# Graph products woven into the start of the attention steps, one probe for the threshold, three blocks ahead instead of four

## Chip, cores and metric

The kernel runs on one core of one Trainium2 chip. The metric is the device time of one execution in microseconds (us), as the median of several runs. The engines are called PE (TensorE, with its weight loads as PEld), DVE (VectorE), ACT (ScalarE), POOL (GpSimd) and SP (SyncE, which here issues DMAs).

## The reference

There are 4096 nodes with 256 features, and a dense 0/1 adjacency matrix `adj` of 4096 x 4096 with about 1.5% ones. Two layers follow each other; each adds its result to its input and works on `h = relu(layernorm(x))`.

Layer 0 is graph attention with four heads: per head `e = leaky_relu(src_i + dst_j)`, masked by `adj`, softmax over j, times the projected features, then a layer norm.

Layer 1 is a diffusion in two steps (`STEPS` = 2), over a fixed graph and over an attention that is recomputed in each step:

```python
R = S + eye; R = R / R.sum(-1)              # S is the adjacency
Xf = Xa = X
for n in range(2):
    A = top_p_attention(Xa, W1, W2, W3)     # 4096 x 4096, row-stochastic
    Xf = R @ Xf                             # "hop" n of the graph products
    Xa = A @ Xa
    Z  = Z + Xf @ U1[n].T + Xa @ U2[n].T
return layernorm(X + Z)
```

`top_p_attention` makes queries and keys of 64 dimensions, logits `q @ k.T`, a softmax, and keeps in every row the largest probabilities until they sum to 0.9 (`TOP_P`); the rest is set to zero and the row is normalized again. No sort is needed: for every row the kernel looks for the threshold above which the kept values hold 0.9 of the sum.

## The kernel before

Rows are worked on in `NB` = 32 blocks of 128. The program goes through these stages one after the other:

1. Layer 0's preparation (normalization, projections, the tiles `parts`, six buffers, stored to `uv_d` by DMAs of ACT's queue) and its 16 passes of masked products. The adjacency is loaded, cut to one byte per entry and kept in `adj_d`. The closing of the last pass's rows is held in a list `later` and laid between the first products of the next stage.
2. The two hops `R @ Xf` (from L431). The result of a hop is made transposed, in four passes of 1024 columns, each over 32 row blocks j; one (pass, j) is a **piece** of eight matmuls (L459). `before_products` prepares a piece two pieces ahead (`LOOK` = 2): a load of `at` (SP, one for two pieces), a DVE cast to `ar` (L445), an ACT copy to `hl` (L451, high part) and a POOL subtraction (L452, low part); `ar` and `hl` have three buffers each. `drained` copies a pass's four accumulators out and stores them by DMAs of ACT's queue to `xft_d`; after hop 0 `by_rows` also turns them back to rows in `xf_d`, the source of hop 1. Both hops are done before step 0 begins.
3. For each of the two steps: `projections` (keys and queries of all blocks; per-row tables such as the mean and spread of the logits, the shift `nm` and the first guess `c1` of the threshold), then the first blocks, then 32 blocks in a loop.

What happens to one block b of a step:

- `began` gives it a tile `e` of 128 x 4096 (five buffers); `logits` (PE, L540) and `exponentials` (ACT, L672) fill it in four chunks and leave the sum of each.
- `first_probe` (ACT, L679, four instructions of 128 x 2048): what lies below `c1`.
- `first_step` (POOL, from L703): some sixteen instructions on single columns, powers among them, make the next guess from the sums and the probe.
- `second_probe` (DVE pass over the block, L734, and POOL instructions from L735), in step 0 only: a second guess corrected by a secant.
- `third_probe` (DVE pass, L755): what lies below the last guess `c3`, kept in `big`.
- `candidates` (DVE, L768 to L785): the largest values below the guess, 8 of each segment of `big` (16 segments in step 0, 18 in step 1); the threshold is found among the best 48.
- `masked` (DVE pass, L791): values below the threshold become zero.
- `attend` (PE): for eight groups of four, `turn` transposes (L854) and ACT copies to `eT` (L856), then `gather` multiplies with X (L862). Between the groups stand the logits of the block that is `AHEAD` = 4 blocks ahead, its exponentials (groups 0 and 1) and its first probes (groups `PROBED` = 2, 3, 5, 6).
- `finish` (DVE): the block's contribution to Z; in step 1 also the last norm.

The order on PE, DVE, ACT and POOL is written out by hand (`manual_schedule`): each of these engines executes its instructions in the order of the program. In the loop, `chosen_kept(b)` and `attend(b)` alternate:

```python
second_probe(b+1); candidates(b); first_step(b+2)
third_probe(b+1); finish(b-2); masked(b)        # then attend(b)
```

If a row's threshold stays undecided (`questioned` looks at the end of a step), `repaired` does its block again after the step, with a search.

Of the kernel before, what the change touches and what calls it, by code (L numbers as in the profile page):

```python
# [11 lines left out]
F32 = mybir.dt.float32  # L12
# [25 lines left out]
SEG = (16, 18)  # L38
# [5 lines left out]
AHEAD = 4  # L44

PROBED = (2, 3, 5, 6)
# [4 lines left out]
def gat_then_top_p_diffusion(  # L51
# [67 lines left out]
    X = xp.tile([P, NB, D], F32, name="X")  # L119

# [38 lines left out]
    with tc.tile_pool(name="l0", bufs=1) as l0, tc.tile_pool(name="l0s", bufs=2) as l0s, tc.tile_pool(name="l0o", bufs=1) as l0o:  # L159
# [23 lines left out]
        with tc.tile_pool(name="l0r", bufs=3) as rows, tc.tile_pool(name="l0w", bufs=1) as l0w, \  # L183
# [4 lines left out]
            for k in range(KC):  # L188
                for i in range(2):
                    pr = l0w.tile([P, H, HD], F32, name="pr")  # L190
                    nc.vector.tensor_mul(pr, wx[:, k, :D].rearrange("p (h d) -> p h d", h=H),
                                         a_r[:, None, ts(i, HD)].to_broadcast([P, H, HD]))
                    nc.vector.reduce_sum(wx[:, k, ds(D + i * H, H)], pr, axis=AX.X)
            for g in range(NB // 4):
                nc.sync.dma_start(X[:, ts(g, 4), :], x[ts(g, 4 * P), :].rearrange("(b p) d -> p b d", p=P))
            for g in range(NB // 4):
# [5 lines left out]
                for i in range(4):  # L202
# [6 lines left out]
                    hT = rows.tile([P, KC, P], F32, name="hT")  # L209
# [12 lines left out]
                    parts = rows.tile([P, H, 2, W3 + 1], BF16, name="parts", bufs=6)  # L222
# [208 lines left out]
        with tc.tile_pool(name="rp", bufs=2) as rp, tc.tile_pool(name="psr", bufs=1, space=PSUM) as psr, \  # L431
                tc.tile_pool(name="psrt", bufs=2, space=PSUM) as psrt, tc.manual_schedule(engines=every):
            PASSES = NB // G0

            def before_products(hop, p, j, at, rows_):

                q = j % 2
                if q == 0:
                    at[:] = [rp.tile([P, 2, G0 * P], F8, name="at")]
                    nc.sync.dma_start(at[0], adj_d[p, :, ds(j, 2), :])  # L440
                    if hop > 0:
                        rows_[:] = [rp.tile([P, 2, D], F32, name="src")]
                        nc.sync.dma_start(rows_[0], xf_d[ds(j, 2)].rearrange("b p d -> p b d"))
                ar = rp.tile([P, G0 * P], F32R, name="ar", bufs=3)
                nc.vector.tensor_copy(ar, at[0][:, q, :])  # L445
                if j // G0 == p:
                    own = ar[:, ts(j % G0, P)]
                    nc.vector.tensor_tensor(own, own.bitcast(F32), ident, ALU.add)
                src = rows_[0][:, q, :] if hop > 0 else X[:, j, :]
                hl = rp.tile([P, 2, D], F32R, name="hl", bufs=3)  # L450
                nc.scalar.copy(hl[:, 0, :], src)  # L451
                nc.gpsimd.tensor_tensor(hl[:, 1, :], src, hl[:, 0, :].bitcast(F32), ALU.subtract)  # L452
                return ar, hl

            def graph_products(p, j, acc, ar, hl):
                for s in range(KC):
                    for c in range(2):
                        for t in range(2):
                            nc.tensor.matmul(acc[s][c], hl[:, t, ts(s, P)], ar[:, ts(c, 512)],  # L459
                                             start=(j == 0 and t == 0), stop=(j == NB - 1 and t == 1))  # L460

            def drained(hop, p, acc):

                turns = []
                out_ = [rp.tile([P, KC, 512], F32, name="xft") for c in range(2)]
                for s in range(KC):
                    for c in range(2):
                        (nc.vector.tensor_copy if c else nc.scalar.copy)(out_[c][:, s, :], acc[s][c])
                for c in range(2):
                    b = p * G0 + 4 * c  # L470
                    for s in range(KC):
                        nc.scalar.dma_start(xft_d[hop][ds(b, 4), :, s, :].rearrange("b p i -> p b i"),
                                            out_[c][:, s, :].rearrange("p (b i) -> p b i", b=4))

                def by_rows(c, i0):
                    pt = psrt.tile([P, 4, P], F32, name="tp")
                    for i in range(2):
                        for s in range(KC):
                            nc.tensor.transpose(pt[:, KC * i + s, :], out_[c][:, s, ts(i0 + i, P)], ident)
                    row = rp.tile([P, 2, D], F32, name="row")  # L480
                    for i in range(2):
                        b = p * G0 + 4 * c + i0 + i
                        nc.scalar.activation(row[:, i, :], pt[:, ds(KC * i, KC), :].rearrange("p s d -> p (s d)"), AF.Copy,
                                             scale=rinv[:, b:b + 1])
                    nc.scalar.dma_start(xf_d[ds(p * G0 + 4 * c + i0, 2)].rearrange("b p d -> p b d"), row)
                return [lambda c=c, i=i: by_rows(c, i) for c in range(2) for i in (0, 2)] if hop + 1 < STEPS else []

            for hop in range(STEPS):
                at, rows_, ready, turned = [], [], {}, []
                order = [(p, j) for p in range(PASSES) for j in range(NB)]  # L490
                for n in range(len(order) + LOOK):
                    if n < len(order):
# [687 lines left out]
```

## Time and profile before

Three runs gave 3119.67, 3121.46 and 3115.0 us (median 3119.67). The profiled execution took 3115.7 us; its span from the first to the last instruction is 3113.9 us, at a mean granted PE clock of 0.968.

| engine | busy us | share of the span |
|---|---|---|
| PE | 2853.4 | 92% |
| DVE | 2440.7 | 78% |
| ACT | 1882.2 | 60% |
| POOL | 1391.4 | 45% |

| stage | us of the span |
|---|---|
| layer 0, preparation | 0 to 133 |
| layer 0, products | 133 to 857 |
| hop 0 | 857 to 1116 |
| hop 1 | 1125 to 1361 |
| step 0, keys and first blocks | 1361 to 1465 |
| step 0, 32 blocks | 1465 to 2264 |
| step 1, keys and first blocks | 2264 to 2360 |
| step 1, 32 blocks and the end | 2360 to 3114 |

Lines of a profile read as follows. A group or a timeline row names the source line (L459), the operation, the tile written, `<-`, the tiles read, and the shapes (partitions x elements); then the number of instructions. In a timeline the first number is the start in us from the span's start and the second the length; square brackets hold the idle time of the engine before it and what ended it. A row of a stretch has the stretch, its length, then for PE, PEld, DVE, ACT and POOL the busy us and the number of instructions, the granted PE clock, the busy share of the DMA engines and GB/s. In the slices each digit is the busy share of one fortieth of the span in tenths.

### The profile page before, as it was taken

What the parts mean: (1) busy time and instruction counts of PE and PEld (TensorE: products, weight loads), DVE (VectorE), ACT (ScalarE), POOL (GpSimd) and SP (SyncE); (2) the same over time, 40 slices, a digit from 0 to 9 for tenths busy, and PEclk for the clock granted to TensorE, in tenths of its full rate; (3) what the DMA queues carried; (4) which work ended last, traced back from release to release, by engine and by line L of the source; (5) the groups of instructions that cost most, each with busy time, mean ns of one, the idle gap of its engine ahead of it and who ended that gap; (6) DMA issues with size and microseconds to landing.
All of it is one profiled execution on the core that took longest, in us unless ns stands there. A gap on an engine that the chain in (4) does not pass through costs nothing. (4 is left out here: it accounts for less than half of the span.)

```text
span 3113.9 us, 51951 instructions
## 1 busy us (share of the span) xinstructions
PE 2853.4 (92%) x19033; PEld 2508.5 (81%) x19033; DVE 2440.7 (78%) x5138; ACT 1882.2 (60%) x2867; POOL 1391.4 (45%) x2047
## 2 busy tenths in 40 slices
PE   4599999999989999986899999999877999999998
PEld 3499999999968878874788888787766888888886
DVE  6666878677565444456999999999859999999995
ACT  5777776878623222237577777676247777777762
POOL 3200101010044434415888899998305323566660
PEclk9799999999989999997999999999998999999999
DMA  7837547382024335520000000000020000000000
GB/s 170 201 109 139 155 103 178 103 173 93 28 68 134 99 124 160 172 84 5 16 19 19 19 19 20 20 19 18 16 71 6 25 27 26 26 30 23 29 23 21
DMA packets 161439, 217.14 MB, mean 70 GB/s; under 512 B 13840, under 2 KB 130576, under 8 KB 161168
## 3 DMA queue, kind: packets, MB, share of 16 engines
q1 hardware_dynamic: 108512, 173.45, 17.0%
q0 software_dynamic: 16896, 16.78, 6.1%
q10 hardware_dynamic: 35760, 23.42, 2.5%
q8 instruction: 155, 2.54, 0.3%
q14 instruction: 116, 0.95, 0.1%
HBM read 200.69 MB, written 59.05 MB: 83 GB/s over the span
## 5 line engine op out<-in xcount | busy, mean ns | idle before, releaser
L862 PE MATMUL acc<-X,eT 128*128 128x256 f32 x4096 | 962.8, 380 | 0.8 <-ACT eT L856 0.8
L862 PEld LDWEIGHTS acc<-X,eT 128*128 128x128 f32 x4096 | 748.8, 190 | 88.1 <-ACT eT L856 1.2
L317 PE MATMUL acc<-ut,m 128*128 128x195 bf16 (+1 forms) x8192 | 704.2, 248 | 30.5 <-DVE st L333 15.7
L317 PEld LDWEIGHTS <-m 128*128 128x128 fp8e4 x8192 | 702.1, 97 | 32.6 <-issue 30.9
L459 PE MATMUL racc<-ar,hl 128*128 128x512 f32 x2048 | 481.1, 396 | 19.2 <-POOL hl L452 5.5
L679 ACT ACTIVATE void<-e,c 128x2048 int8<-128x2048 f32 x244 | 490.5, 2010 | 0.6
L291 ACT ACTIVATE g<-sr,d_big 128x1024 uint8<-128x1024 f32 x448 | 471.9, 1137 | 14.5 <-DMA uv_d<-parts 10.1
L459 PEld LDWEIGHTS racc<-ar,hl 128*128 128x128 f32 x2048 | 389.0, 191 | 106.1 <-ACT hl L451 8.6
L672 ACT ACTIVATE e<-mm,nm 128x1024 f32<-128x1024 f32 x256 | 285.9, 1117 | 304.7 <-PE mm L540 301.1
L856 ACT COPY eT<-tp 128x512 f32<-128x512 f32 x512 | 298.6, 583 | 160.1 <-PE tp L854 159.3
L854 PE MATMUL tp<-ident,e 128*128 128x128 f32 x2048 | 314.1, 277 | 80.2 <-DVE e L791 78.1
L854 PEld LDWEIGHTS tp<-ident,e 128*128 128x128 f32 x2048 | 252.7, 142 | 148.2 <-issue 69.9
L445 DVE CAST ar<-at 128x1024 fp32r<-128x1024 fp8e4 x256 | 184.2, 720 | 235.9 <-PE racc L459 233.8
L768 DVE MAX8 cand<-big 128x8 f32<-128x228 f32 (+1 forms) x1088 | 343.9, 395 | 0.1
L297 DVE TENSOR_TENSOR m<-g,ax 128x512 uint32<-128x512 uint32 x256 | 177.0, 691 | 161.3 <-PE acc L317 131.8
L755 DVE SCALAR_TENSOR_TENSOR big<-e,lowered 128x4096 f32<-128x4096 f32 x64 | 287.2, 4488 | 16.5 <-POOL lowered L700 16.5
L791 DVE SCALAR_TENSOR_TENSOR e<-e,found 128x4096 f32<-128x4096 f32 x64 | 287.5, 4492 | 0.0
L540 PE MATMUL mm<-kT,qT 128*128 128x512 f32 x512 | 206.9, 486 | 32.0 <-ACT e L672 31.5
L452 POOL TENSOR_TENSOR hl<-X,hl 128x256 fp32r<-128x256 f32 x128 | 99.9, 783 | 256.9 <-ACT hl L451 256.8
L298 DVE TENSOR_TENSOR m<-m,ax 128x512 uint32<-128x512 uint32 x256 | 178.1, 696 | 26.0 <-DVE m L297 0.9
L172 POOL DMA_DIRECT2D ax<-in_adj_t_dram x32 | 24.8, 777 | 357.7 <-DVE m L298 346.2
L709 POOL TENSOR_TENSOR sums<-sums 128x4 f32<-128x4 f32 (+1 forms) x64 | 19.6, 306 | 359.3 <-ACT void L679 217.2
(230 smaller groups left out, 3753.6 us busy)
## 6 DMA issues: line engine op xcount, KB each, us to landing
ut<-uv_d SPq DMA_DIRECT2D x60, 784.0 KB, 4.5
at<-adj_d SPq DMA_DIRECT2D x128, 256.0 KB, 2.7
ax<-in_adj_t_dram POOLq DMA_DIRECT2D x32, 512.0 KB, 14.7
adj_d<-ax SPq DMA_DIRECT2D x32, 512.0 KB, 6.9
src<-xf_d SPq DMA_DIRECT2D x64, 256.0 KB, 2.9
uv_d<-parts ACTq DMA_DIRECT2D x32, 294.0 KB, 5.0
xft_d<-xft ACTq DMA_DIRECT2D x32, 256.0 KB, 4.1
xf<-xft_d SPq DMA_DIRECT2D x64, 128.0 KB, 2.0
```

Of the source, the lines that this page charges most:

```text
L291: nc.scalar.activation(g[:, c, :], shared[k].sr, AF.Relu, scale=BIG, bias=d_big[:, h, j:j + 1])
L317: nc.tensor.matmul(shared[k].acc[i][:, t, :cols], m[t][:, c, ts(i, P)], shared[k].ut[j // QUARTER][:, j % QUARTER, t, :cols], start=(j == ...
L459: nc.tensor.matmul(acc[s][c], hl[:, t, ts(s, P)], ar[:, ts(c, 512)], start=(j == 0 and t == 0), stop=(j == NB - 1 and t == 1))
L540: nc.tensor.matmul(pm[:, h, :], q[t], kT[:, ds(h * (N // 2) + c * 512, 512)], start=(t == 0), stop=(t == 1))
L672: nc.scalar.activation(ev[:, :, c, :], r.pm[c], AF.Exp, bias=r.nm, accum_out=r.sums[:, c // 2, c % 2:c % 2 + 1])
L679: nc.scalar.activation(void, r.e[:, ts(h, N // 2)], (AF.Relu, AF.Sign)[i], bias=r.c1, scale=-1.0, accum_out=r.sums[:, h, 2 + i:3 + i])
L755: nc.vector.scalar_tensor_tensor(big, r.e, r.c3, r.e, ALU.is_le, ALU.mult, accum_out=r.L)
L768: nc.vector.max(cand[:, s, :], big[:, edges[s]:edges[s + 1]])
L791: nc.vector.scalar_tensor_tensor(r.e, r.e, r.t, r.e, ALU.is_ge, ALU.mult, accum_out=kept)
L854: nc.tensor.transpose(pt[:, i, :], r.e[:, ts(4 * g + i, P)], ident)
L856: nc.scalar.copy(eT, pt)
L862: nc.tensor.matmul(r.acc[:, 0, :], eT[:, i, :], cur[:, j, :], start=(j == 0), stop=(j == NB - 1))
```

## The change

- **Weaving.** `hops(hop)` is now a generator that yields after every piece. Hop 0 starts as before (22 pieces, with `later` between them). Its other 106 pieces run in step 0's own hand-written order: after each piece comes one part of `fills` (`projections` cut into 34 parts, then logits, exponentials, first probes and `first_step` of blocks 0 to 2) and one part of `picks` (third probe, candidates and mask of these blocks, once they have stepped). Hop 1 is woven in the same way into step 1; the loads of X for step 1 follow its first four pieces.
- **Buffers and queues of the hops.** The accumulators now come from the steps' PSUM pools (one of the two buffers of the logits and both of `acc`). `hl` has two buffers instead of three. The stores of `drained` and `by_rows` and the loads of the U weights move from ACT's queue to SP's; hop 1's source rows are loaded one block at a time. SP is among the engines in written order.
- **Single probe.** `second_probe` and its secant go. In step 0 the first guess is corrected from the block's own sum (`summed`, five POOL instructions after the exponentials) before the first probe uses it, and `first_step` has 22 POOL instructions in step 0 and 17 in step 1. Step 0 takes 18 segments too.
- **Three blocks ahead.** `AHEAD` 4 to 3, `e` tiles five to four, `PROBED` 2, 3, 5, 6 to 3, 4, 5, 6.
- `parts` in layer 0's preparation has four buffers instead of six; two small tiles move to another pool. `questioned` has one more test.

```diff
-SEG = (16, 18)
+SEG = 18
-AHEAD = 4
-PROBED = (2, 3, 5, 6)
+AHEAD = 3
+PROBED = (3, 4, 5, 6)
...
-                    parts = rows.tile([P, H, 2, W3 + 1], BF16, name="parts", bufs=6)
+                    parts = rows.tile([P, H, 2, W3 + 1], BF16, name="parts", bufs=4)
...
-                hl = rp.tile([P, 2, D], F32R, name="hl", bufs=3)
+            hl = rp.tile([P, 2, D], F32R, name="hl")
...
+        def hops(hop):
+            at, ready, turned = [], {}, []
+            order = [(p, j) for p in range(PASSES) for j in range(NB)]
+            for n in range(len(order) + LOOK):
+                if n < len(order):
+                    ready[n] = before_products(hop, *order[n], at)
+                if n >= LOOK:
+                    p, j = order[n - LOOK]
+                    if j == 0:
+                        wide = ps2.tile([P, 2, 512], F32, name="mm")
+                        acc = [[wide[:, s, :] for s in range(KC)],
+                               [ps1.tile([P, 2, D], F32, name="acc").rearrange("p t d -> p (t d)") for s in range(KC)]]
+                    graph_products(j, acc, *ready.pop(n - LOOK))
+                    if turned and j >= 2:
+                        turned.pop(0)()
+                    if j == NB - 1:
+                        turned = drained(hop, p, acc)
+                    yield
...
+        with tc.manual_schedule(engines=every | {ET.SP}):
+            for n in range(NB - G0 - LOOK):
+                next(first_hop)
+                if later:
+                    later.pop(0)()
...
+    def summed(r):
+        s = r.sums
+        pool.tensor_tensor(s[:, 0, :2], s[:, 0, :2], s[:, 1, :2], ALU.add)
+        pool.tensor_scalar(r.z, s[:, 0, 0:1], s[:, 0, 1:2], None, ALU.add)
+        if r.n == 0:
+            one = slice(r.b, r.b + 1)
+            up, c1 = col("pulled", 2), col("c1x", 6)
+            pool.tensor_scalar(up, r.z, r.G.level[:, one], None, ALU.mult)
+            pool.tensor_tensor(up, up, r.G.pull[:, one], ALU.pow)
+            pool.tensor_scalar(c1, up, r.c1, 2.5e30, ALU.mult, ALU.min)
+            r.c1 = c1
...
@@ attend @@
             if g < 2:
                 start(2 + g)
+                if g == 1 and ahead:
+                    summed(ahead)
             elif g in PROBED and ahead:
                 first_probe(ahead, PROBED.index(g))
...
+    def fills(n, G, found, blocks):
+        weights(n)
+        yield from projections(X, n, G)
+        swaps[0] = swapped(G.qT[:, ts(0, P)])
+        for b in range(AHEAD + 1):
+            if b < AHEAD:
+                r = blocks[b] = began(n, b, G)
+                for c in range(4):
+                    r.pm = {c: logits(r.q, r.kT, c)}
+                    exponentials(r, c)
+                    yield
+                summed(r)
+                yield
+            if b > 0:
+                for i in range(4):
+                    first_probe(blocks[b - 1], i)
+                    yield
+                first_step(blocks[b - 1])
+                yield
+
+    def picks(n, found, blocks):
+        for b in range(AHEAD):
+            while b not in blocks or not hasattr(blocks[b], "stepped"):
+                yield
+            r = blocks[b]
+            for i in range(6 if b == 0 else 0):
+                yield
+            third_probe(r)
+            for i in range(3):
+                yield
+            yield from searching(r, found)
+            yield
+            masked(r)
+            r.kept = True
+            for i in range(3):
+                yield
...
+            pieces = first_hop if n == 0 else hops(n)
+            filling, picking = fills(n, G, found, blocks), picks(n, found, blocks)
+            if n > 0:
+                for i in range(4):
+                    next(pieces)
+                for g in range(NB // 4):
+                    nc.sync.dma_start(cur[:, ts(g, 4), :], xa_d[ts(g, 4)].rearrange("b p d -> p b d"))
+            for _ in pieces:
+                next(filling, None)
+                next(picking, None)
...
             def chosen_kept(b):
                 r = blocks[b]
...
-                if not early and b < NB - 1:
-                    second_probe(blocks[b + 1])
...
-                if b + 2 < NB:
+                if b + 2 < NB and not hasattr(blocks[b + 2], "stepped"):
                     first_step(blocks[b + 2])
-                if b + 1 < NB:
+                if b + 1 < NB and not hasattr(blocks[b + 1], "thirded"):
                     third_probe(blocks[b + 1])
```

## The prediction

> **What bounds the kernel now.** I read the page's 40 slices first (77.85 us each), to find the stages:
>
> ```profile
> PE   4599999999989999986899999999877999999998
> DVE  6666878677565444456999999999859999999995
> POOL 3200101010044434415888899998305323566660
> ```
>
> TensorE (PE) dips three times after the start: where hop 0 begins (slice 11), before the blocks of step 0 (18) and before those of step 1 (28 to 30). In step 0 (19 to 27) DVE and POOL are full too. Then busy time by stretch (us; PE, PEld, DVE, ACT, POOL, granted clock, DMA):
>
> ```profile
> 916.00:1116.00 200.00, 199.57 (x906) 164.77 (x905) 100.92 (x138) 56.83 (x136) 81.11 (x104) 1.00 0.35 107
> 1116.00:1361.00 245.00, 237.42 (x1032) 194.44 (x1032) 113.98 (x167) 59.66 (x144) 97.22 (x128) 0.98 0.49 154
> 1361.00:1465.00 104.00, 65.56 (x421) 53.98 (x421) 68.69 (x117) 64.16 (x99) 34.78 (x59) 0.82 0.09 25
> 1550.00:2264.00 714.00, 663.34 (x3476) 571.38 (x3475) 677.49 (x1435) 460.49 (x690) 592.13 (x800) 0.99 0.06 19
> 2264.00:2360.00 96.00, 66.18 (x433) 53.63 (x431) 60.43 (x116) 52.78 (x88) 15.19 (x30) 0.87 0.19 60
> 2437.00:3019.00 582.00, 580.63 (x3049) 498.73 (x3047) 562.04 (x1406) 434.04 (x650) 300.02 (x474) 1.00 0.09 26
> ```
>
> In order: the last 106 pieces of hop 0, hop 1, keys and first blocks of step 0, its blocks, keys and first blocks of step 1, its blocks. Hops and step 1 are PE at work; the two preludes leave PE idle for 38 and 30 us; step 0 is DVE's (677 of 714). By the first transposes of each block (L854, timeline) a block takes 24.88 us in step 0 and 23.29 in step 1.
>
> Then one block of step 0 in the timeline, POOL beside DVE:
>
> ```profile
> 1714.63 4.48 DVE L755 SCALAR_TENSOR_TENSOR big<-e,lowered 128x4096 f32<-128x4096 f32 x1
> 1714.68 4.84 POOL L699 TENSOR_TENSOR lowered<-inv_e,a 128x1 f32<-128x1 f32 x1
> ...
> 1719.63 0.26 POOL L700 TENSOR_SCALAR lowered<-lowered,c 128x1 f32<-128x1 f32 x1
> 1719.85 0.20 POOL L719 TENSOR_TENSOR yy<-a 128x1 f32<-128x1 f32 x1
> 1719.90 4.47 DVE L791 SCALAR_TENSOR_TENSOR e<-e,found 128x4096 f32<-128x4096 f32 x1
> 1720.00 4.78 POOL L720 TENSOR_TENSOR up<-z,mone 128x1 f32<-128x1 f32 x1
> ```
>
> The power of one column (L720) takes 0.56 us in step 1 at 2601.58 and 4.78 here: a POOL instruction that meets DVE's pass over a whole block waits until the pass ends. This row carries the forecast.
>
> **Step 0, block by block.** Out goes the second probe, one DVE pass (4.41 start to next start): DVE then has 24.88 - 4.41 + 0.1 for two more maxima (16 take 5.32, 18 take 5.43) = 20.6 us, under PE's 23.29. By these sums alone a block would take PE's 23.29. But a new wait comes in. In step 0 the first probe's bias (ACT) is now made on POOL by `summed` from the block's own exponentials, and POOL keeps the written order: `first_step` of block k+2, then `summed` of k+3, then `first_step` of k+3, which needs the four probes. So POOL and ACT form a ring that must close once per block. Three blocks ahead instead of four adds the other half: the third probe of k+2 now comes just before the mask of k+1, and DVE, which has time to spare, starts it the moment `first_step` delivers.
>
> One turn, from E, the end of a block's probes (it lies at the start of the next `attend`):
> - `first_step` of k+2: 22 instructions at 0.41, the pitch of the 16 from 2621.74 to 2628.28 in step 1: E to E+9.1.
> - third probe of k+2, a whole pass: to E+13.5. The exponentials of k+3 end 12.3 us after `attend` starts (step 1: logits at 2598.60, exponential 2609.68 to 2610.88), inside it: `summed` is locked out.
> - two small DVE instructions of `finish`, 0.86 (1719.04 to 1719.90): room for about two of `summed`'s five. Then the mask of k+1, a pass to E+18.8: its power is locked out.
> - power and product after the lock, 1.2 us: E+20.0.
> - four probes on ACT with eT copies between. Pitch 2.47 and 2.0 + 0.1 for the last:
>
> ```profile
> 2611.25 2.01 ACT L679 ACTIVATE void<-e,c 128x2048 int8<-128x2048 f32 x1
> ...
> 2613.25 0.58 ACT L856 COPY eT<-tp 128x512 f32<-128x512 f32 x1
> 2613.72 2.02 ACT L679 ACTIVATE void<-e,c 128x2048 int8<-128x2048 f32 x1
> ```
>
> 3 x 2.47 + 2.1 = 9.5, so the next E is E+29.6. Behind the waiting probe on ACT stand the copies of eT for groups 5 to 7; PE has work up to group 4 only (17.8 us into `attend`) and waits some 5 us for each block. Blocks 0 to 2 come finished out of the weaving, so the ring runs for `attend` 2 to 28: 27 x 29.6 = 799. `attend` 0 has no pass in its way (23.5), `attend` 1 meets one (25.7), the last three have no logits (23.29 - 3.4 = 19.9 each, 60). Together 908, against 799 now (1465.1 to the last gather's end at 2264.3): **+109**.
>
> PE's waits cost clock as well. Rows after an idle time of 5.53 us and with the clock up:
>
> ```profile
> 2364.63 3.78 PE L862 MATMUL acc<-X,eT 128*128 128x256 f32 x8 [0.80 <-ACT eT L856]
> 2370.07 1.89 PE L862 MATMUL acc<-X,eT 128*128 128x256 f32 x8
> ```
>
> After step 0's present waits of 1.7 to 1.9 us the transposes take 0.63 against 0.60. A wait of 5 us is like the first: one or two slow gathers put the next `attend` back by 2 us or so, its exponentials fall into the mask's pass, and all five of `summed` come after it, 2.1 instead of 1.2: a turn of 30.5 at most. I keep 29.6 as the copies, not PE, end the turn; 30.5 (+24) goes into the range.
>
> The Trainium skill, "TensorE: Matmul & The Clock Gate", Part 1, says that a window of about 3.4 us without work brings the array to half clock, and that as long a busy one is needed to come back. By that rule each block of step 0 would start its last three gathers at half clock, an estimate of up to 3 x 1.73 = 5 us of PE per block, on top of the wait. It speaks against any change that puts a 5 us hole into every block.
>
> **The weaving, hop 0 with step 0.** PE's work stays and is only laid in sequence. After the unchanged first 22 pieces (to 916): 199.6 for 106 pieces; keys 44 (PE from 1361.7 to 1411.1, less a DMA wait of 5.6); 12 logits chunks at 1.0 (0.86 in step 1, 1.17 at 1411.12) = 12; 256 against 304 now (916 to 1465), -48. Against that, with `hl` in two buffers POOL's subtraction (0.76) must follow ACT's copy (0.41) within one piece of 1.815 us, so any hold on POOL is a hold on PE:
> - three `first_step` in POOL's queue ahead of the next subtraction: 9.0 + 0.76 less the pieces already prepared and logits between, some 6.5 each: 20.
> - six passes (third probe and mask of three blocks), each locking out a subtraction for 4.41 less about 2 of cover: 2.5 each, 15.
> - twelve probes of 2.2 on ACT beside `hl` copies, 2.6 per piece against 1.8 on part of them: 5.
> - SP's queue, now in written order: the row stores of hop 0 (32, and 16 of xft, which leave ACT's queue) wait for ACT's copies ahead of the next load of `at` (2.7 us to land, cast 0.69). Up to 1.3 eight times, 10; some is covered by logits: 3. The weights' and swapped queries' loads land long before use.
> Together -5; between -48 (all covered) and +15.
>
> **Hop 1 with step 1.** Now: 245 + 96 = 341. Then: 6 from the last gather to the first piece, 236 + 44 + 12, 5 for X's eight 512 KB loads standing ahead of `at` on SP, three `first_step` of 17 instructions (6.9 us, 4.5 each) 13, passes 15, probes 5: 336, **-5** (bounds -45 and +15).
>
> **The rest.** Step 1: its four first block times are 28.8, 24.7, 23.3 and so on, 7 us over PE's pace, which goes; 3.4 comes back as one more block has its logits in `attend`; with the probes at groups 3 to 6 the copy of eT for group 7 lands within 0.1 us of PE's need, 3: 0. In step 1 the ring isn't closed (the bias is ready), and `first_step` delivers at 7 us into `attend` where DVE needs it. Four buffers of `parts` instead of six: POOL waits for them 32.1 us in 12 times now, with DMA busy 0.72 to 0.90 in these slices: 0 to 8, I take 2.
>
> **Sum.** On the profiled execution, 3115.7 (span 3113.9, 1.8 around it; the three runs' median is 3119.67, within 3115.0 to 3121.5): +109 - 5 - 5 + 0 + 2 = 3217. Taken for the runs: **3218**.
>
> **Rivals.**
> 1. *PE sets step 0* (faster). If `summed` gets through before DVE's passes, because POOL or DVE stands otherwise than I lay it out, all 29 blocks with logits take 23.29: 29 x 23.29 + 60 = 735, -64, in all 3044; with the weaving's holds covered as well, 2970. For: DVE's 20.6 and PE's 580.6 of 582 in step 1. Against: the 4.78 rows. It decides once the bias comes within 14 us of `attend`'s start. 0.22.
> 2. *One pass locks, not two*: bias at E+15.7, a turn of 25.2; step 0 then 790, -9: 3099. Against: only 0.86 us between the passes for five instructions. 0.08.
> 3. *The weaving is worse*: passes and `first_step` fall together and PE runs cold in between: both ends +15, SP's 10 uncovered, turn 30.5: 3290. 0.06.
> 4. *The single probe does not do what it says*: rows left undecided are redone after the step. No such block ran (L791 x64). One costs about 45 (logits and exponentials 10, a block 23, its end), 140 more if searched (31 passes by the code at 4.5): 3265 to 3400. 0.04.
>
> The forecast has 0.60. Likeliest alone: 3175 to 3265. The range must take in rival 2 and part of 1, so 3010 to 3270. About 0.2% is what a measurement of this kernel can tell from no change: faster 0.29, same 0.02, slower 0.69.
>
> **What would show it.** Right: blocks of step 0 at 29 to 31 us, ACT's first probe there waiting about 6 us for POOL, PE's waits for ACT's eT copies summing to over 100 us, POOL's new power at over 4 us, DVE waiting on POOL before each third probe; hops without seams but with PE waits for `hl` of 6 us, three in each. Wrong: block times of 23.3 in step 0 with ACT's probe on time (rival 1), an L791 count over 64 (rival 4), or prelude savings of 40 each.

## The result, and the profile after

The changed kernel took **3282.9 us** (median of four runs, 3282.0 to 3289.5) against 3118.3 us for the kernel before in the same session: 1.0533 times as long, 95% interval 1.0514 to 1.0551. Forecast were 3218 and a range of 3010 to 3270. The side was right; the time is 65 us over the forecast and 13 us over the range. The profiled execution took 3282.1 us, its span 3279.9, against a span of 3113.9 before: 166 us more.

By stages, from the starts of the pieces and of each block's first transposes in the timelines (step 0 ends with its last gather):

| stretch | before | after | more | forecast |
|---|---|---|---|---|
| start to first piece of hop 0 | 857.5 | 854.9 | -2.6 | +2 |
| its first 22 pieces | 58.8 | 59.4 | +0.6 | 0 |
| rest of hop 0, keys and first blocks of step 0 (without hop 1) | 303.8 | 340.5 | +36.7 | -5 |
| step 0, 32 blocks | 799.2 | 893.8 | +94.6 | +109 |
| hop 1, keys and first blocks of step 1 | 340.9 | 376.8 | +35.9 | -5 |
| step 1, 32 blocks and the end | 753.7 | 754.5 | +0.8 | 0 |

So the ring of step 0 is there, some 14 us shorter than forecast. What was missed, by 83 us together, are the two woven stretches. The 40 slices of the page (82 us each here) show both:

```profile
PE   5699999999899589888988888989779999999998
DVE  6667768677554573776666776735573799999996
POOL 3200101010223633444444444212552323232332
PEclk8799999999999799899999989999889999999999
```

Counted from 0, step 0 fills slices 16 to 25: no engine is full there any more, neither PE (8 in most of them) nor DVE (6 or 7 in most) nor POOL (4 or less). That is how a ring of waits looks. The dips of PE are now in slice 13, inside woven hop 0, and in slices 28 and 29, inside woven hop 1, each with a lower granted clock.

One block of step 0 from the timeline after, around the waits:

```profile
1514.13 4.48 DVE L762 SCALAR_TENSOR_TENSOR big<-e,c 128x4096 f32<-128x4096 f32 x1 [8.41 <-POOL c L756]
...
1518.34 0.32 POOL L714 TENSOR_TENSOR sums<-sums 128x2 f32<-128x2 f32 x1 [4.25 <-ACT e L701]
...
1518.77 0.29 POOL L715 TENSOR_SCALAR z<-sums 128x1 f32<-128x1 f32 x1
1519.15 0.29 POOL L719 TENSOR_SCALAR pulled<-z,level 128x1 f32<-128x1 f32 x1
1519.39 4.47 DVE L804 SCALAR_TENSOR_TENSOR e<-e,found 128x4096 f32<-128x4096 f32 x1
...
1519.53 4.76 POOL L720 TENSOR_TENSOR pulled<-pulled,pull 128x1 f32<-128x1 f32 x1
...
1524.39 0.30 POOL L721 TENSOR_SCALAR c1x<-pulled,c 128x1 f32<-128x1 f32 x1
1524.72 2.00 ACT L708 ACTIVATE void<-e,c1x 128x2048 int8<-128x2048 f32 x1 [4.42 <-POOL c1x L721]
...
1527.34 3.48 PE L875 MATMUL acc<-X,eT 128*128 128x256 f32 x8 [3.38 <-ACT eT L869]
...
1531.08 3.62 PE L875 MATMUL acc<-X,eT 128*128 128x256 f32 x16
```

Read down, this is one turn. `first_step` began at 1505.43 and ended 8.7 us later; DVE had waited 8.41 us for it and starts the third probe at once. `summed` of the next block is released by the block's exponentials (ACT L701) shortly before that pass ends. Its first instruction (L714, at 1518.34) lasts until the pass is over, two more follow before the mask starts, and its power (L720) lies under the mask for 4.76 us. So of the two passes the mask costs the most: over the 28 turns of the ring L714 takes 0.75 us on the mean and the power 4.6, against 0.20 and 0.58 in the run with the added wait below, where no pass stands beside them. Only then does ACT get its bias, 19.3 us after `first_step` began (20.0 forecast). Behind ACT's probe stands the copy of `eT`, for which PE waits 3.38 us; the gather after that is slow (3.48 us for eight), the next is not (3.62 us for sixteen).

Over the whole run, first the groups after, then the same groups in the run with one added wait on DVE that the next section opens with. The columns after the bar are busy time, mean ns of one, and idle time just before with what ended it. (The 32 powers of L720 include those of the first blocks, which met no pass.)

```profile
L762 DVE SCALAR_TENSOR_TENSOR big<-e,c 128x4096 f32<-128x4096 f32 x64 | 287.8, 4497 | 302.7 <-POOL c L756 268.7 <-POOL c L753 33.7 <-issue 0.2
L708 ACT ACTIVATE void<-e,c1x 128x2048 int8<-128x2048 f32 x128 | 256.6, 2005 | 131.7 <-POOL c1x L721 131.6
L720 POOL TENSOR_TENSOR pulled<-pulled,pull 128x1 f32<-128x1 f32 x32 | 132.0, 4125 | 2.7
L875 PE MATMUL acc<-X,eT 128*128 128x256 f32 x4096 | 1012.4, 394 | 103.6 <-ACT eT L869 103.5
```

```profile
L762 DVE SCALAR_TENSOR_TENSOR big<-e,c 128x4096 f32<-128x4096 f32 x64 | 287.6, 4493 | 33.9 <-POOL c L753 33.7 <-issue 0.2
L708 ACT ACTIVATE void<-e,c1x 128x2048 int8<-128x2048 f32 x128 | 256.7, 2005 | 3.1
L720 POOL TENSOR_TENSOR pulled<-pulled,pull 128x1 f32<-128x1 f32 x32 | 18.7, 585 | 2.7
L875 PE MATMUL acc<-X,eT 128*128 128x256 f32 x4096 | 971.8, 381 | 4.2 <-ACT eT L869 0.8
```

In the second list the power takes 585 ns instead of 4125, ACT no longer waits for the bias, and PE no longer waits for `eT`; PE's gathers are 40.6 us shorter as well. The granted clock over step 0's blocks is 0.92 in the changed kernel (1300 to 2090 us) and 1.00 with the wait (1300 to 1930 us).

### The profile page after: what moved, and what is told of

It is laid out like the page before. It is cut to its first block, busy times and chain, and to the rows that moved or that the text cites. A ratio compares the mean times of both kernels' runs of the same rounds, so it can differ in the third digit from the quotient of the medians.

```text
span 3279.9 us, 52140 instructions
## 1 busy us (share of the span) xinstructions
PE 2935.2 (89%) x19033; PEld 2548.9 (78%) x19033; DVE 2290.9 (70%) x5143; ACT 1897.7 (58%) x2892; POOL 1015.1 (31%) x2053
## 5 line engine op out<-in xcount | busy, mean ns | idle before, releaser
L875 PE MATMUL acc<-X,eT 128*128 128x256 f32 x4096 | 1012.4, 394 | 103.6 <-ACT eT L869 103.5
L875 PEld LDWEIGHTS acc<-X,eT 128*128 128x128 f32 x4096 | 776.0, 198 | 215.3 <-ACT eT L869 120.7
L762 DVE SCALAR_TENSOR_TENSOR big<-e,c 128x4096 f32<-128x4096 f32 x64 | 287.8, 4497 | 302.7 <-POOL c L756 268.7
L701 ACT ACTIVATE e<-mm,nm 128x1024 f32<-128x1024 f32 x256 | 286.8, 1120 | 294.5 <-PE mm L549 282.7
L467 PE MATMUL mm<-ar,hl 128*128 128x512 f32 x1024 | 311.7, 426 | 110.1 <-POOL hl L460 55.3
L708 ACT ACTIVATE void<-e,c1x 128x2048 int8<-128x2048 f32 x128 | 256.6, 2005 | 131.7 <-POOL c1x L721 131.6
L467 PEld LDWEIGHTS mm<-ar,hl 128*128 128x128 f32 x1024 | 197.2, 203 | 166.6 <-POOL hl L460 64.1
L467 PE MATMUL acc<-ar,hl 128*128 128x512 f32 x1024 | 296.1, 413 | 4.4 <-DVE eT L476 3.2
L804 DVE SCALAR_TENSOR_TENSOR e<-e,found 128x4096 f32<-128x4096 f32 x64 | 286.9, 4484 | 0.0
L708 ACT ACTIVATE void<-e,c 128x2048 int8<-128x2048 f32 x128 | 257.5, 2012 | 0.0
L467 PEld LDWEIGHTS acc<-ar,hl 128*128 128x128 f32 x1024 | 205.8, 201 | 54.4 <-DVE eT L476 5.1
L460 POOL TENSOR_TENSOR hl<-x,hl 128x256 fp32r<-128x256 f32 x128 | 112.9, 884 | 285.1 <-ACT hl L459 285.1
```

The costliest lines, as they stand in the source:

```text
L467: nc.tensor.matmul(acc[c][s], hl[:, t, ts(s, P)], ar[:, ts(c, 512)], start=(j == 0 and t == 0), stop=(j == NB - 1 and t == 1))
L701: nc.scalar.activation(ev[:, :, c, :], r.pm[c], AF.Exp, bias=r.nm, accum_out=r.sums[:, c // 2, c % 2:c % 2 + 1])
L708: nc.scalar.activation(void, r.e[:, ts(h, N // 2)], (AF.Relu, AF.Sign)[i], bias=r.c1, scale=-1.0, accum_out=r.sums[:, h, 2 + i:3 + i])
L762: nc.vector.scalar_tensor_tensor(big, r.e, r.c3, r.e, ALU.is_le, ALU.mult, accum_out=r.low3)
L804: nc.vector.scalar_tensor_tensor(r.e, r.e, r.t, r.e, ALU.is_ge, ALU.mult, accum_out=kept)
L875: nc.tensor.matmul(r.acc[:, 0, :], eT[:, i, :], cur[:, j, :], start=(j == 0), stop=(j == NB - 1))
```

## The experiments

All are edits of the changed kernel (3282.9 us). Where a stretch is named, hop 0's is from piece 22, hop 1's from its first piece, both to the hop's last matmul (330.3 and 368.5 us in the changed kernel) unless the first block is named as its end.

### The ring of step 0: one wait in the right place

```diff
                 if b + 1 < NB and not hasattr(blocks[b + 1], "thirded"):
+                    if n == 0 and b + 2 < NB:
+                        nc.vector.tensor_scalar(col("seen", 2), blocks[b + 2].c1, 1.0, None, ALU.mult)
                     third_probe(blocks[b + 1])
```

A single-column DVE instruction reads the corrected guess of the block after next, so DVE's pass can't start before POOL has made it. It adds a wait and removes nothing.

> One DVE instruction more in step 0: before the third probe of block k+2, DVE reads the corrected bias of block k+3, so it waits for the five POOL instructions of `summed` and its two passes come after them. Ring theory (POOL's `summed`, locked out by DVE's passes, closes a ring with ACT's probes of 29.0 us per block): the bias is ready 14.4 us after E instead of 19.3, a block of step 0 takes 14.4 + 9.5 = 23.9, 27 blocks x 5.1 = 138 us less, 3145 us; the power in `summed` falls from 4.1 us to under 1. Rival (the turn is set by ACT's own four probes in a row, by DVE's wait for the last guess, or by PE's half clock): an added wait on DVE puts the mask 5 us later and can only cost: 3283 to 3420.

Measured: **3135.1 us** (3131.6 to 3139.1), ratio to before 1.0065 (1.0048 to 1.0082): 148 us less than the changed kernel. Blocks of step 0 take 23.55 us instead of 29.05 on the mean (784.5 over the 27 turns of `attend` 2 to 28); 27 x 5.5 = 148.5 is the whole gain. From the timeline of one block:

```profile
1501.24 0.57 POOL L720 TENSOR_TENSOR pulled<-pulled,pull 128x1 f32<-128x1 f32 x1
1501.91 0.30 POOL L721 TENSOR_SCALAR c1x<-pulled,c 128x1 f32<-128x1 f32 x1
1502.24 0.15 DVE L1137 TENSOR_SCALAR seen<-c1x 128x1 f32<-128x1 f32 x1 [2.64 <-POOL c1x L721]
1502.24 2.00 ACT L708 ACTIVATE void<-e,c1x 128x2048 int8<-128x2048 f32 x1
1502.31 4.47 DVE L762 SCALAR_TENSOR_TENSOR big<-e,c 128x4096 f32<-128x4096 f32 x1
```

DVE waits 2.64 us for the guess and starts its pass 0.07 us after ACT's probe. DVE has less than a block's time of work, so these 2.64 us cost nothing.

### The same ring without the correction

The five instructions of `summed` shrink to two: the guess comes from the table, as in step 1. This run leaves out the correction of the first guess in step 0 and the redoing of undecided rows.

```diff
-        if r.n == 0:
+        if False:
             one = slice(r.b, r.b + 1)
             up, c1 = col("pulled", 2), col("c1x", 6)
...
```

> Step 0 leaves out the correction of the first guess: the first probe's bias comes from the table, as in step 1, and POOL's three instructions for it go (one clamp comes into `first_step`); blocks left undecided are not redone, so that only the wait is taken out. Ring theory: nothing on ACT waits for POOL, a block of step 0 takes PE's 23.3 to 23.5: 27 x 5.6 = 151 less, 3132 us. Rival (ACT's bunched probes or DVE's wait for POOL's last guess set the turn): blocks stay at 28 to 29, 3265 to 3283.

Measured: **3129.1 us** (3125.0 to 3132.5), ratio 1.0041 (1.0027 to 1.0056), blocks of 23.4 us. Two ways of opening the ring, one by making DVE wait and one by taking the bias off POOL, give nearly the same pace (23.55 and 23.4). The ring is the cause of step 0's time.

### `first_step` in parts between the pieces

`stepping` is `first_step` with five yields in it, so that a piece of the hop lies between each two of its six parts.

```diff
...
-                first_step(blocks[b - 1])
+                yield from stepping(blocks[b - 1])
                 yield
```

> In the weaving alone, `first_step` is cut into six parts with a piece of the hop between them; the loop is unchanged. Theory (in the preludes POOL's long runs stand ahead of the next subtraction for `hl`, PE waits and then runs at half clock): PE's waits for `hl` of 31 and 22 us fall below 15 each, 30 to 50 us less in all: 3235 to 3255. Rival (what costs there is DVE's passes, or loads of `at` behind stores on SP): 0 to -10, 3273 to 3283.

Measured: **3248.3 us** (3242.8 to 3251.8), ratio 1.0425 (1.0407 to 1.0442): 35 less. Hop 0's stretch to the first block shrinks from 340.5 to 318.7 (-22), hop 1's stretch from 368.5 to 351.2 (-17). The price of an undivided `first_step` is seen in the changed kernel's timeline, at that of block 2 (the last in the stretch):

```profile
1133.80 4.48 DVE L762 SCALAR_TENSOR_TENSOR big<-e,c 128x4096 f32<-128x4096 f32 x1
1134.03 4.93 POOL L736 TENSOR_SCALAR den<-den,c1x 128x1 f32<-128x1 f32 x1
...
1145.55 1.41 POOL L460 TENSOR_TENSOR hl<-X,hl 128x256 fp32r<-128x256 f32 x2
1146.33 1.65 PE L467 MATMUL mm<-ar,hl 128*128 128x512 f32 x3 [10.44 <-POOL hl L460]
```

This `first_step` began at 1131.39. The pass at 1133.80 is block 1's third probe, which `picks` lays beside it; one of the 22 instructions, beside it, takes 4.93 us, so that the subtractions for the next pieces come 14.2 us after the start, and PE stands for 10.44.

### Three buffers of `hl`

```diff
-            hl = rp.tile([P, 2, D], F32R, name="hl")
+            hl = rp.tile([P, 2, D], F32R, name="hl", bufs=3)
```

(The room comes from sharing four small tiles that are not in use at the same time.)

> `hl` in three buffers again (room is made by letting four small tiles of other stages use the same pool). Theory (POOL's holds are met with only one piece of slack): one piece more, 1.8 us at each of some 18 holds, and less half clock: 20 to 40 us less, 3245 to 3263. Rival (the written order puts the next subtraction behind the hold whatever the buffers): 0 to -8, 3275 to 3283.

Measured: **3268.8 us** (3265.9 to 3270.6), ratio 1.0487 (1.0470 to 1.0505): 14 less, between the two expectations. PE's waits for POOL's subtraction in hop 0's stretch only go from 31.3 to 28.4 us. One more prepared piece is worth 1.8 us, the time of a piece, and PE's waits in the third part of that stretch are 2 to 10 us long.

### The row stores back on ACT's queue

```diff
-                    nc.sync.dma_start(xft_d[hop][ds(p * G0 + 4 * c, 4), :, s, :] ...
+                    nc.scalar.dma_start(xft_d[hop][ds(p * G0 + 4 * c, 4), :, s, :] ...
...
-                    nc.sync.dma_start(xf_d[b], row)
+                    nc.scalar.dma_start(xf_d[b], row)
```

> The stores of drained and by_rows go back from SP's queue to ACT's; all else as in the changed kernel (3282.9). Theory (SP's written order is a small part of the weaving's price: 3 us were put down for each hop, 10 at most; what holds PE is POOL's and DVE's work between the pieces): 3270 to 3284. Rival (the loads of at standing behind row stores on SP carry the excess of about 40 us in each woven stretch): 3250 to 3262, and DVE's waits in ar for at (31.4 us in 9 times in the first woven stretch) nearly gone.

Measured: **3270.0 us** (3268.3 to 3273.7), ratio 1.0489 (1.0471 to 1.0506): 13 less, at the theory's lower end. DVE's waits for `at` in hop 0 vanish altogether, as the rival said, and yet the hop is hardly shorter: piece 22 to the first block takes 339.5 us instead of 340.5, as PE's waits for POOL's subtraction grow. First the waits of hop 0's stretch in the changed kernel, then in this run (us in total, times, longest):

```profile
DVE ar L454 <- DMA at<-adj_d: 31.4, 9, 6.9
PE mm L467 <- POOL hl L460: 31.3, 6, 10.4
PE mm L467 <- DVE ar L454: 18.7, 11, 3.7
```

```profile
PE mm L467 <- POOL hl L460: 37.8, 10, 12.2
PE mm L467 <- DVE ar L454: 6.0, 4, 3.5
```

Taking one hold away lets the next one show. The 13 us came from hop 1, whose stretch goes from 368.5 to 354.0.

### No picks between the pieces, then the stores on ACT as well

With `first_step` in parts, `picks` (third probe, maxima and mask of the first three blocks) is moved behind the hop:

```diff
             for _ in pieces:
                 next(filling, None)
-                next(picking, None)
             for _ in filling:
-                next(picking, None)
-            for _ in picking:
                 pass
+            third_probe(blocks[0])
```

> first_step in six parts with a piece between them, and nothing of picks (third probe, maxima, mask of the first three blocks) between the pieces; those are done in the loop, which therefore starts later and with more work: about +30 us in step 0 and +20 in step 1. Read by the stretches from piece 22 of hop 0, and from the start of hop 1, to the hop's last matmul: 330 and 375 us in the changed kernel, 308 and 358 with first_step in parts alone. Theory (first_step and the passes are what holds the pieces): 270 to 290 and 325 to 340. Rival (ACT's exponentials and probes, SP or the loads hold as much): over 297 and over 348. The whole 3240 to 3275 by the theory.

Measured: **3252.7 us** (3251.0 to 3253.7), ratio 1.0435 (1.0418 to 1.0453). The stretches are 286 and 326 us, as the theory said: 22 and 25 us less than with `first_step` in parts alone. The whole is 4 us slower, because the time comes back later, most of it before the loop's first block. There PE now waits for block 0's mask (L814 in this run; L877 is the first transposes), once before step 0 and once before step 1:

```profile
1227.62 1.09 PE L877 MATMUL tp<-ident,e 128*128 128x128 f32 x4 [16.01 <-DVE e L814]
...
2492.74 1.12 PE L877 MATMUL tp<-ident,e 128*128 128x128 f32 x4 [24.41 <-DVE e L814]
```

With `first_step` in parts alone these waits aren't there. In step 0 the first two blocks also take 32.2 and 29.8 us instead of 23.6 and 24.7, at the pace of the closed ring from the start; in step 1 the loop is only some 2 us longer.

What the passes cost inside the hop is seen in the third part of hop 0's stretch, as idle time and as clock. First the changed kernel (pieces 64 to 95), then this run:

```profile
1049.00:1166.00 117.00, 79.12 (x294) 60.89 (x293) 59.53 (x129) 46.22 (x78) 66.21 (x108) 0.82 0.18 56
```

```profile
1050.00:1130.60 80.60, 70.29 (x293) 53.57 (x293) 29.69 (x42) 44.24 (x74) 48.10 (x85) 0.98 0.26 80
```

The same 294 and 293 matmuls take 79.1 us of PE's time at a granted clock of 0.82, and 70.3 at 0.98. Of the 36.4 us between the two, 27.6 are PE standing (37.9 against 10.3) and 8.8 PE at a lower clock.

> As the run with first_step in parts and no picks between the pieces (3252.7; 286 us from piece 22 to the hop's last matmul in hop 0, 326 in hop 1), with the stores of drained and by_rows on ACT's queue again. In that run DVE's cast of ar still waited 42.7 us for loads of at, which stand behind row stores on SP, and PE waited 10 us for the cast. Theory (with POOL's and DVE's holds gone, SP's written order is what is left): 270 to 278 and 312 to 320, the whole 3230 to 3242. Rival (the stores only move the hold to ACT, whose queue they then enter, so the earlier small gain of 13 us is all or more than there is): 280 to 290 and 320 to 330, the whole 3245 to 3258.

Measured: **3243.2 us** (3241.6 to 3249.4), ratio 1.0405 (1.0388 to 1.0423), between the two expectations. The stretches agree with one each: 286 in hop 0 is the rival's, where nothing is gained though no wait for `at` is left, and 313 in hop 1 is the theory's, where 13 us go.

### No weaving at all

```diff
             for _ in pieces:
-                next(filling, None)
-                next(picking, None)
+                pass
```

> All pieces of a hop run first, then fills and picks, in the same written order otherwise; buffers, queues, the ring of step 0 and the three blocks ahead stay. It prices the weaving as a whole. Theory (the weaving costs what it was measured above the separate stages: +37 and +36 us): 3210 to 3235, with piece 22 to the first block of step 0 at 300 to 315 us (340 now) and hop 1 with its first blocks at 340 to 355 (376 now). Rival (the weaving gains, and the extra time of the two stretches comes from the changed buffers, queues and POOL work, which stay here): 3280 to 3330.

Measured: **3324.9 us** (3324.0 to 3329.4), ratio 1.0670 (1.0652 to 1.0688): 42 *more* than the changed kernel, so the theory fell. The weaving gains. Piece 22 to the first block takes 357 us here, 340.5 woven, 304 in the kernel before. The order without weaving is not the kernel before: a pass of 32 pieces takes 69.7 us instead of 60.0, and what follows the hop takes 130 instead of 104 (keys and first blocks of step 0). The seam at a pass's end, from this run's timeline:

```profile
1002.18 1.11 SPq L477 DMA_DIRECT2D xft_d<-stage  x2
...
1003.34 1.15 SPq L477 DMA_DIRECT2D xft_d<-eT  x2
...
1004.54 1.69 SPq L447 DMA_DIRECT2D at<-adj_d  x2
...
1008.39 1.90 DVE L454 CAST ar<-at 128x1024 fp32r<-128x1024 fp8e4 x3 [4.91 <-DMA at<-adj_d]
```

SP issues the loads of `at` only after the four stores, in the written order, and DVE waits 4.91 us for them.

> As the unwoven run (3324.9; 69.7 us for the 32 pieces of a pass in hop 0, 65.5 in hop 1, against 60.0 and 58.3 in the kernel before), with the stores of drained and by_rows on ACT's queue again. Theory (a load of at behind the stores of a pass's end costs 7 to 10 us for each pass of an unwoven hop): 59 to 62 us for a pass in both hops, the whole 3265 to 3288. Rival (the seam at the end of a pass comes from the accumulators in the steps' PSUM pools or from hl in two buffers): 66 to 70, the whole 3310 to 3325.

Measured: **3303.7 us** (3303.1 to 3306.5), ratio 1.0596 (1.0579 to 1.0614): 21 less than unwoven and between the two expectations, so SP's order is a real seam, but not the whole of it. A pass takes 65.9 and 65.3 us in hop 0 (the rival's number, nearly) and 60.2 and 61.9 in hop 1 (the theory's). What is left in hop 0's seams is PE's wait for the accumulators to be copied out (5.7 us in three times) and smaller waits. I did not take them apart.

### Putting the parts together

The wait on DVE, `first_step` in parts and three buffers of `hl`:

> Three things at once: DVE waits for the next block's corrected guess before its third probe (opens the ring, -148 us by itself), first_step in six parts (-35 by itself), three buffers of hl (-14 by itself). Theory (the ring and the weaving's holds add up, the last two overlap in part): 3085 to 3100, which is under the kernel before (3118). Rival (what first_step in parts frees is taken by the DVE passes once hl is deeper, so the last two give no more than one of them): 3100 to 3112.

Measured: **3081.3 us** (3075.5 to 3083.9), ratio to before 0.9879 (0.9862 to 0.9896). That is 4 us under the theory's range: the three gains add up (148 + 35 + 14 = 197, and 202 measured), and this kernel is faster than both. With the stores on ACT's queue too:

> The combination that gave 3081.3 (DVE's wait for the corrected guess, first_step in six parts, three buffers of hl) with the stores of drained and by_rows on ACT's queue too. Theory (with the other holds shortened, SP's order comes to the front, and freeing it gives 5 to 15 us): 3066 to 3077. Rival (passes and POOL hold the pieces at the same places anyway): 3078 to 3086.

Measured: **3083.0 us** (3080.4 to 3084.9), ratio 0.9883 (0.9866 to 0.9899): no gain, the rival's answer. Last, the first combination with only block 0 picked between the pieces:

```diff
     def picks(n, found, blocks):
-        for b in range(AHEAD):
+        for b in range(1):
```

> The combination that gave 3081.3 (DVE waits for the corrected guess, first_step in six parts, three buffers of hl), with only block 0's third probe, maxima and mask between the pieces; those of blocks 1 and 2 are done in the loop. With the ring open DVE has 20.6 us of work in a block of 23.5, so the loop can take them. Theory (picks of three blocks hold the pieces for 22 and 25 us, so two thirds of that come free): 3045 to 3064, with piece 22 to the first block at 300 to 306 (317 there) and hop 1 with its first blocks at 350 to 358 (371). Rival (the loop's first blocks wait for DVE and give it back, as when no block was picked): 3070 to 3088.

Measured: **3057.5 us** (3052.7 to 3058.6), ratio **0.9801** (0.9785 to 0.9817), the fastest of all. Piece 22 to the first block takes 296 us; hop 1, counted as for that number from the first transposes of step 0's last block, 354. From its page:

```profile
PE   4699999999989988999999999889899999999997
DVE  6666877767655555888888888555649999999996
PEclk7799999999999999999999999999999999999999
```

Step 0 (slices 16 to 25 of 76 us each) has PE at 9 in all but the last, with DVE at 8 in most, and no clock digit under 9 after the start. Against the same kernel with all picks woven, piece 22 to the first block is 21 us shorter and hop 1 with its first blocks 17, and the loops are no longer in step 0 and 3 us longer in step 1: DVE has the time for these picks there. Two things differ from the run without picks, which gained nothing. Block 0 is still picked between the pieces, so that PE no longer waits 16 and 24 us for its mask; and the ring of step 0 is open. In step 1, where the bias comes from the table and no ring is closed in any of these runs, the first is what makes the difference. How much the second adds in step 0 was not measured apart.

## Why the prediction was right and wrong

**Step 0: right in mechanism, 14 us too large.** Each turn had all its steps in the forecast order. Two terms were off. `first_step` took 8.7 us, not 9.1: its 22 instructions stand closer than the pitch of 0.41 that was taken from a row of step 1. And from the end of the mask to ACT's probe it is 0.86 us, not 1.2, as the power ends 0.43 us after the mask and only the product follows. The bias came at 19.3 us instead of 20.0. The listed terms also add up to 29.5, not 29.6 (20.0 + 9.5). A turn took 29.05; over 27 turns that makes the 14. PE's 103.5 us of waits for `eT`, POOL's power at over 4 us and DVE's waits for `first_step` were as listed beforehand; ACT's waits were 4.7 us on the mean (131.6 over 28), not about 6.

The Trainium skill, "SBUF — State Buffer", section "Who interferes with whom", says that VectorE and GpSimd share a port pair, and that a VectorE instruction with two SBUF inputs contends with a GpSimd instruction that reads SBUF. Here the two inputs of L804 and L762 are the same tile, and the power of one column took 4125 ns on the mean of 32, nearly all beside such a pass; with the pass held back, 585. Trace and page agree, and the two inputs need not be two tiles.

The clock rule weighed in the prediction ("TensorE: Matmul & The Clock Gate", Part 1) gave up to three slow gathers and 5 us in each block. The trace has one slow group of eight after a wait of 3.38 us, and the gathers lose 40.6 us over the run or 1.5 in a block. The granted clock in that block, in two stretches (the row's last three numbers are clock, DMA share and GB/s):

```profile
1526.95:1530.37 3.42, 3.04 (x7) 2.50 (x8) 3.35 (x15) 3.42 (x5) 0.00 (x0) 0.50 0.00 0
1530.37:1553.00 22.63, 21.88 (x116) 18.57 (x115) 14.04 (x28) 11.79 (x20) 13.01 (x26) 1.00 0.07 21
```

The half clock began 3.0 us into the wait and lasted 3.42 us, and one group of eight fell into it. The trace's record of the clock has one such stretch in each of the 27 blocks, of 3.4 us in 18 and of 6.8 in nine. That is near the rule, with one window or two, and under the estimate of three slow gathers in each block that was made from it.

**The weaving: the failed step.** The step that failed is the price of the holds between woven pieces. The forecast took PE's own work as a floor (256 us in hop 0) and put 43 us of holds on it. The measured stretch is 340.5, so 84 stand on the floor. The runs give their sizes, in the order in which they were taken away (another order could divide them otherwise):

- `first_step` in POOL's queue: 22 us in hop 0, 17 in hop 1 (20 and 13 forecast). That term was nearly right, as a sum, 6 us too small over both.
- Passes and the rest of `picks`: 22 and 25 (15 and 15 forecast). Only the six passes' lock on POOL had been priced. The same DVE queue also holds the cast to `ar`, for which PE waited 18.7 us in hop 0. And the holds meet: a pass inside a `first_step` made PE stand for 10.44 us where 6.5 was the price of one.
- The clock after a hold was left out of the weaving, though the prediction had priced it for step 0. Within the two terms above it is some 9 us of pieces 64 to 95 alone.
- What is left in hop 0 with all that gone: from 256 to 286, and the seam from the last matmul to the first block, 10.1 in the changed kernel. This seam was dropped from the sum, although rows must still be turned after the last piece: PE's transposes there wait 4.90 us for ACT's `xa`. With the seam, 40 us stand here against 8 forecast (probes 5, SP 3). In the run with the stores on ACT, PE is busy for 262 of the 286; the other 24 are many small waits (7.5 for POOL's subtraction in 12 times, 5.5 for the accumulators). They were not taken apart further, so their cause stays open.
- SP's order: no gain in hop 0 while woven, 13 in hop 1 (where none was priced for the stores), though 21 in the unwoven order.

Hop 1 divides in the same way: from PE's 292 us (236 + 44 + 12) to the 368.5 measured there are 17 for `first_step`, 25 for the picks, 13 for the stores on SP and 21 left over, which stay open too; forecast were 13, 15, nothing and 10 (X's loads and the probes).

The bound of +15 for each end was therefore too tight. Rival 3 had named the right mechanism (passes and `first_step` fall together, PE cold in between, 3290) and had been given 0.06. That its number lies so near to the 3282.9 is luck: its ends were too cheap (+15 each against +37 and +36), and its turn of 30.5 in step 0 did not come.

**What the weaving replaced was mis-seen too.** The comparison was made with the stages of the kernel before. The change also alters these stages: unwoven, its hop and prelude take 357 us, not 304. Of the 53 us, 27 lie in the hop and its seams (227 us for 106 pieces instead of 200) and 26 in what follows it, where PE waits 22.2 us for the mask before the loop can start. The weaving gains 17 us of them back, measured against its own parts.

**The rest.** Step 1 came out at +0.8 (0 forecast), layer 0 at -2.6 (+2 forecast, bounds 0 to 8). In the runs with the same layer 0 the first piece starts at 853.0 to 858.6 us, so that four buffers of `parts` cost nothing that can be told from this spread. No block was redone (L804 x64).

## What to carry to other kernels

When a small instruction on one engine feeds an engine that everyone waits for, look at what else may run at that time: an engine with slack that starts its long pass as early as it can may close a ring, and making it *wait* can be the remedy (here one instruction, 148 us). When work is woven into a PE-bound stage, price each inserted piece by how long it holds the queues that prepare the next piece, against how much is prepared ahead; cut long runs of instructions into parts shorter than that, and add the PE time at the lower clock after each hold. Work that some later stage has room for need not be woven in, except what that stage must have to start: the best version weaves in the picks of the first block alone.

## What the runs showed of the hardware that I had not expected

- POOL's instruction on a single column that began under a DVE pass (1518.34) ended 0.05 us after it (1518.66). In the gap up to the next pass at 1519.39 two more started; the one after them started 0.14 us after that pass and lasted 4.76 us, to 0.43 us after its end.
- A wait of 3.38 us slowed one group of eight gathers (3.48 us against 1.89), with the granted clock at 0.50 for 3.42 us, and the next sixteen were back at full pace (3.62).
- In the third part of woven hop 0 (1049 to 1166 us) PE's waits of 4.3, 5.4, 8.6 and 10.4 us ended at 1081, 1100, 1120 and 1146 us, with two of some 2 us beside them; the mean granted clock of these 117 us is 0.82.
